# Folded bias vectors of an attention layer: weighted sums over weight chunks on VectorE, one product with ones per output chunk on TensorE

## The chip, the cores and the metric

The kernel runs on one core of one Trainium2 chip. A core has TensorE (PE, matrix products; its weight loads are shown as PEld), VectorE (DVE), ScalarE (ACT), GpSimd (POOL) and SyncE (SP, which here only issues DMAs). The metric is the device time of one launch in microseconds (us). Everything is float32 unless said otherwise.

## The reference

The input x is 8 images of 512 channels by 32 x 32 pixels. Four layers follow each other, each with a residual; only what bears on the change is given.

- Layer 0: an attention over 64 channels, whose score matrix is divided by its largest singular value sigma. Then `conv1x1(z2, Wv, bv) + x`.
- Layer 1, the layer of the change:

```
h = group_norm(x) * gamma + beta
q = wq h + bq;  k = wk h + bk;  v = wv h + bv
out = wp (v softmax(q^T k / sqrt(512))^T) + bp
x = x + out
```

- Layer 2: an attention with 128 channels. Layer 3: a product of signs with sign weights, batch norm and a leaky rectifier.

All weight matrices of layer 1 are 512 x 512, the biases have 512 entries.

## The kernel before

**Folding.** Layer 1 needs neither q nor v. The kernel makes two products of weights, `wu` (from wq and wk) and `wo` (from wv and wp), so that scores are h^T (wu h + bu) and the output is wo h weighted by the softmax, plus bo. The folded biases are `bu` = wk^T bq and `bo` = wp bv + bp, each a vector of 512 held as a tile of 128 partitions by 4 chunks. `bvo` is `bo` plus layer 0's bias.

**Stages.** Up to about 100 us all images are loaded and projected for layer 0 (L1241), weights are turned (`natural`, L1201) and statistics taken. From then to about 194 us one pair of images gets its sigma, by a power iteration (`chain`, L1020 and L1021: two products of 128x128, each result evicted half by DVE, L1036 or L1042, half by ACT, L1034 or L1038; every third step a trace is summed: L1047, L1048 on DVE, a product L1052, and a reciprocal L1075). When it ends (`td`, ln and exp on ACT at L1096 and L1099, each with a load of its table), the pair's weights are made (L287), and the first image goes through `entering(0)`: four visits (L409 on PE; L418, L421 and L423 on DVE), then the group norm's means and variances (L430, L437), the reciprocal root with GpSimd (L232), `normal` (L460) and `split_h` (L324 to L327). The rest of the time to the end is the eight images' main work, from `make_u` on (L385).

**What fills the gaps.** Between the steps of that chain PE does other work, from the generator `filler` (L1411): the product `wu` (L1281), grams of the other three pairs (L1328, after transposes L1133 that are evicted by DVE at L1139 and ACT at L1137), the folded biases (`biases`, L1297), and last the product `wo` (L1281 again, 16 products of 128x512, evicted at L1294). The loop at L1443 takes so many items from the filler at each step of the chain, and the loop at L1450 so many at each visit:

```
    for n in (2, 3, 3, 3, 3, 4, 6):
        next(steps)
        for _ in range(n):
            next(todo, None)
```

PE's order is that of the program there (`manual_schedule`); the other engines' order is set by a planner. Each engine works its own queue in that order. `biases` runs inside the filler, one item after each item of the grams (L1427).

**How a bias is made before.** For each of the four output chunks, four products with a moving operand of one column add up over the four input chunks in one PSUM bank (L1306); DVE then copies the column (L1314) or adds bp (L1316). That is 16 products for bu and 16 for bo.

PSUM in this stage has two double banks (`wide`) and four single ones (`bank`), shared by the chain, the transposes, the visits and the biases.

Of the kernel before, what the change touches and what calls it, by code (L numbers as in the profile page):

```python
# [8 lines left out]
F32 = mybir.dt.float32  # L9
# [3 lines left out]
ALU = mybir.AluOpType  # L13
# [3 lines left out]
P = 128  # L17
B = 8
C = 512
N = 1024  # L20
CC = C // P
# [64 lines left out]
def kernel(  # L86
# [17 lines left out]
    nc = tc.nc  # L104
    mm = nc.tensor.matmul
# [17 lines left out]
    def bank():  # L123
        return psum["bank"].tile([P, HF], F32, tag="bank", name="bank")
# [25 lines left out]
    sbw = {}  # L150

    def load_w(name, src, shape, pool=wpool, eng=nc.sync, tag=None):
        t = pool.tile(shape, F32, tag=tag or name, name=name)
        eng.dma_start(out=t, in_=src)
        sbw[name] = t
        return t
# [4 lines left out]
    a1 = early.enter_context(tc.tile_pool(name="a1", bufs=1))  # L161
# [28 lines left out]
        nc.vector.tensor_tensor(fold[:, i, :], ident[:, 0:MID], ident[:, MID:P], ALU.add)  # L190
    nc.vector.tensor_scalar(fold, fold, 0.5, None, ALU.mult)
    fold = fold.rearrange("p g j -> p (g j)")

    ct = const.tile([P, NCOL], F32, tag="ct", name="ct")
    nc.scalar.dma_start(out=ct, in_=cols)
# [2 lines left out]
    bvc = const.tile([P, CC], F32, tag="bvc", name="bvc")  # L198
# [21 lines left out]
    def vec(name):  # L220
        return ct[:, COL[name] : COL[name] + CC]

    def col(name, i):
        return ct[:, COL[name] + i : COL[name] + i + 1]

    def rsqrt_eps(pool, var, n, name):

        v = pool.tile([P, n], F32, tag=name + "_v", name=name + "_v")
        r = pool.tile([P, n], F32, tag=name + "_r", name=name + "_r")
        e = pool.tile([P, n], F32, tag=name + "_e", name=name + "_e")  # L230
        nc.vector.tensor_scalar(v, var, EPS, None, ALU.add)
        nc.gpsimd.tensor_tensor(r, v, minus_half[:, 0:n], ALU.pow)  # L232
        nc.vector.tensor_tensor(e, r, r, ALU.mult)
        nc.vector.tensor_tensor(e, e, v, ALU.mult)
        nc.vector.tensor_scalar(e, e, -0.5, 1.5, ALU.mult, ALU.add)
        nc.vector.tensor_tensor(r, r, e, ALU.mult)
        return r
# [23 lines left out]
    bu = const.tile([P, CC], F32, tag="bu", name="bu")  # L261
    bo = const.tile([P, CC], F32, tag="bo", name="bo")
# [890 lines left out]
        return absw[:, 0, :]  # L1153

    def scale_signs(total):
        ones = a1.tile([P, 1], F32, tag="ones", name="ones")
        nc.vector.memset(ones, 1.0)
        ps = bank()
        for oc in range(CC):
            mm(  # L1160
                out=ps[:, oc : oc + 1],
                lhsT=total[:, bass.ts(oc, P)],
                rhs=ones,
                start=True,
                stop=True,
            )


        a = rsqrt_eps(a1, vec("L3_conv_bn_var"), CC, "r3")
        nc.vector.tensor_tensor(a, a, vec("L3_conv_bn_gamma"), ALU.mult)  # L1170
        nc.vector.tensor_tensor(cb3, a, vec("L3_conv_bn_mean"), ALU.mult)
        nc.vector.tensor_tensor(cb3, vec("L3_conv_bn_beta"), cb3, ALU.subtract)
        nc.vector.tensor_tensor(cb3, cb3, vec("L3_conv_pr_shift"), ALU.subtract)
        nc.vector.scalar_tensor_tensor(sa3, ps[:, 0:CC], 1.0 / C, a, ALU.mult, ALU.mult)
        a = rsqrt_eps(a1, vec("L2_conv_bn_var"), CC, "r2")
        nc.vector.tensor_tensor(inv2, a, vec("L2_conv_bn_gamma"), ALU.mult)
        nc.vector.tensor_tensor(bb2, inv2, vec("L2_conv_bn_mean"), ALU.mult)
        nc.vector.tensor_tensor(bb2, vec("L2_conv_bn_beta"), bb2, ALU.subtract)

        nc.vector.tensor_tensor(rb3, vec("L3_conv_rsign_bias"), bb2, ALU.add)  # L1180
        nc.vector.tensor_tensor(cb3, cb3, bb2, ALU.add)
        slope = vec("L3_conv_pr_slope")
        nc.vector.tensor_scalar(ps3, slope, -1.0, 1.0, ALU.mult, ALU.add)
        nc.vector.tensor_tensor(pb3, slope, cb3, ALU.mult)
        nc.vector.tensor_tensor(pb3, pb3, vec("L3_conv_pr_bias"), ALU.add)
        nc.vector.tensor_scalar(nc3, cb3, -1.0, None, ALU.mult)
        nc.vector.tensor_tensor(qb3, cb3, vec("L3_conv_pr_bias"), ALU.add)

    def scale_z():

        rep = a1.tile([P, CC, P], F32, tag="absw", name="rep")
        nc.vector.tensor_copy(rep, inv2.unsqueeze(2).to_broadcast([P, CC, P]))
        ps = bank()
        for oc in range(CC):
            mm(out=ps[:, bass.ts(oc, P)], lhsT=rep[:, oc, :], rhs=ident, start=True, stop=True)
        nc.vector.tensor_tensor(sbw["z"], sbw["z"], ps, ALU.mult)


    nat = {}

    def natural(name, tag):  # L1201
        t = nat[name] = a1.tile([P, CC, C], F32, tag=tag, name="nat_" + name)
        for i in range(CC // 2):
            tp = wide().rearrange("p (o c j) -> p o c j", o=2, j=P)
            for k in range(2):
                for cc in range(CC):
                    nc.tensor.transpose(
                        tp[:, k, cc, :], sbw[name][:, cc, bass.ts(2 * i + k, P)], ident
                    )
            dst = t[:, 2 * i : 2 * i + 2, :].rearrange("p o (c j) -> p o c j", j=P)  # L1210
            nc.scalar.copy(dst[:, 0], tp[:, 0])
            nc.vector.tensor_copy(dst[:, 1], tp[:, 1])
            yield
# [62 lines left out]
    def product(lt, rhs, dst, vector):  # L1276
        for i in range(CC // 2):
            ps = wide()
            for k in range(2):
                for oc in range(CC):  # L1280
                    mm(  # L1281
                        out=ps[:, half(k)],
                        lhsT=lt[:, oc, bass.ts(2 * i + k, P)],
                        rhs=rhs[:, oc, :],
                        start=oc == 0,
                        stop=oc == CC - 1,
                    )
                    if k == 0 or oc < CC - 1:
                        yield
            to = dst[:, 2 * i : 2 * i + 2, :].rearrange("p o c -> p (o c)")  # L1290
            if i % 2 and vector:
                nc.vector.tensor_copy(to, ps)
            else:
                nc.scalar.copy(to, ps)  # L1294
            yield

    def biases():  # L1297

        for w, rhs, dst in (
            (nat["k"], [col("L1_conv_bq", k) for k in range(CC)], bu),  # L1300
            (sbw["p"], [bvc[:, k : k + 1] for k in range(CC)], bo),
        ):
            for i in range(CC):
                ps = bank()
                for k in range(CC):
                    mm(  # L1306
                        out=ps[:, 0:1],
                        lhsT=w[:, k, bass.ts(i, P)],
                        rhs=rhs[k],
                        start=k == 0,  # L1310
                        stop=k == CC - 1,
                    )
                if dst is bu:
                    nc.vector.tensor_copy(bu[:, i : i + 1], ps[:, 0:1])  # L1314
                else:
                    nc.vector.tensor_tensor(  # L1316
                        bo[:, i : i + 1], ps[:, 0:1], col("L1_conv_bp", i), ALU.add
                    )
                yield
        nc.vector.tensor_tensor(bvo, bo, vec("L0_conv_bv"), ALU.add)  # L1320


# [2 lines left out]
    def gram(j, i, lt, rhs):  # L1325
        ps = wide()
        for t in range(NT):
            mm(  # L1328
                out=ps[:, 0:P],
                lhsT=lt[:, t, :],  # L1330
                rhs=rhs[:, t, :],
                start=t == 0,
                stop=t == NT - 1,
            )
            if t == NT // 2 - 1:
                yield
        nc.vector.tensor_tensor(gm[j][:, i, :], ps[:, 0:P], mask2, ALU.mult)
        yield
# [30 lines left out]
    ps = bank()  # L1369
# [5 lines left out]
    ps = bank()  # L1375
# [35 lines left out]
    def filler():  # L1411

        yield from natural("v", "k")
        load_w("p", w_p, [P, CC, C], a1, tag="v")
        yield from product(nat["q"], nat["k"], wu, True)
        yield from gram(jl, 2, ht_pair[jl], gtl)
        scale_z()
        yield  # L1420
        between = biases()
        sums = sums_u()
        for j in rest:
            for _ in grams(j):
                next(sums, None)
                yield
                if next(between, "end") != "end":  # L1427
                    yield
        yield from product(nat["v"], sbw["p"], wo, False)

    todo = filler()
    for _ in range(5):
        next(todo)
# [215 lines left out]
```

## Time and profile before

| | us |
|---|---|
| median of 4 runs (1914.26 to 1915.22) | 1914.88 |
| the profiled execution | 1914.82 |
| its span, first to last instruction | 1913.0 |
| busy time of PE / DVE / ACT / POOL | 1891.7 / 1126.3 / 510.3 / 224.3 |
| granted TensorE clock, mean | 0.999 |

The stage around the change, by stretches of the trace (busy us of each engine):

| from to | PE | PEld | DVE | ACT | POOL |
|---|---|---|---|---|---|
| 134.4 to 158.7 | 22.56 | 21.48 | 13.28 | 5.84 | 0.00 |
| 158.7 to 187.0 | 26.89 | 17.66 | 17.46 | 4.37 | 0.00 |
| 187.0 to 198.5 | 10.82 | 4.73 | 9.81 | 2.61 | 1.02 |
| 198.5 to 221.0 | 22.50 | 9.56 | 7.44 | 3.33 | 2.53 |

A line of the chain of waits reads: start in us, length, engine, tile, line, and how many records. A line of the timeline reads: start, length, engine, line, operation, out<-in, count; in brackets, how long the engine had been idle before it and what released it. A float32 product has two records (two passes), a float32 transpose one. The ends of matmul records are modelled, and neighbours overlap; the start-to-start distance is the time that one takes from PE.

### The profile page before, as it was taken

The page shows a single profiled execution, that of the slowest core. Times are in us where ns is not written, and L with a number is a line of the kernel's source. Part 1 is how long each engine was busy: PE and PEld are TensorE (multiplying, and loading weights), DVE is VectorE, ACT ScalarE, POOL GpSimd, SP SyncE. Part 2 cuts the span into 40 slices and gives each one's busy share as a digit, 9 for nine tenths or more (in the row PEclk, how much of TensorE's full clock was granted, in tenths as well). Part 3 has the DMA queues.
Part 4 walks back from the last instruction along what each step waited for, and adds up shares of the span by engine and source line. Part 5 has one row for each costly group of instructions (what it writes and reads, how often), then busy time and mean ns, then how long its engine had stood idle before and what let it go on. Part 6 is the DMA issues. An engine that isn't in the chain of part 4 may idle for free.

```text
span 1913.0 us, 16430 instructions
## 1 busy us (share of the span) xinstructions
PE 1891.7 (99%) x6166; PEld 982.2 (51%) x6166; DVE 1126.3 (59%) x1761; ACT 510.3 (27%) x811; POOL 224.3 (12%) x175
## 2 busy tenths in 40 slices
PE   9999999999999999999999999999999999999997
PEld 3366456544655447454645446544645455544653
DVE  3245677448664677447764676447753775466547
ACT  2141221135212332125212331034202521234014
POOL 0000001200121011200121011201120011101121
PEclk9999999999999999999999999999999999999999
DMA  8420000002000120002000120002000200010001
GB/s 319 159 78 7 0 6 12 1 12 88 17 1 0 33 72 12 0 12 88 17 1 0 34 72 12 1 12 88 11 1 5 94 12 0 0 34 22 12 1 46
DMA packets 27782, 66.45 MB, mean 35 GB/s; under 512 B 4272, under 2 KB 5424, under 8 KB 27056
## 3 DMA queue, kind: packets, MB, share of 16 engines
q1 hardware_dynamic: 26768, 64.90, 10.1%
q8 instruction: 50, 0.82, 0.2%
q10 hardware_dynamic: 864, 0.43, 0.1%
q14 instruction: 36, 0.29, 0.0%
q0 software_dynamic: 64, 0.00, 0.0%
HBM read 38.51 MB, written 18.87 MB: 30 GB/s over the span
## 4 chain that ended last, share of the span: by engine, by line
PE 92%; DVE 6%; issue 1%; ACT 1%; DMA 0%; POOL 0%; DVEq 0%; ACTq 0%
PE bank L385 42%; PE bank L554 20%; PE bank L949 6%; PE bank L803 6%; PE bank L1241 5%; PE bank L655 3%; PE bank L409 2%; PE bank L672 2%; PE wide L1281 1%; DVE both L746 1%; PE wide L1328 1%; DVE both L716 1%; PE bank L1020 1%; PE bank L1021 1%; PE bank L695 1%; PE bank L824 1%
## 5 line engine op out<-in xcount | busy, mean ns | idle before, releaser
L554 PE MATMUL bank<-e,vt 128*128 128x512 f32 x768 | 334.2, 593 | 0.0
L554 PEld LDWEIGHTS bank<-e,vt 128*128 128x128 f32 x768 | 144.9, 190 | 174.8 <-issue 173.1
L385 PE MATMUL bank<-ut,h 128*128 128x512 f32 x384 | 182.3, 597 | 0.0
L342 DVE TENSOR_TENSOR e<-bank,e 128x512 f32<-128x512 f32 x128 | 87.8, 686 | 81.9 <-PE bank L385 81.7
L385 PE MATMUL bank<-us,hs 128*128 128x512 f32 x256 | 121.5, 597 | 1.3 <-DVE us L314 0.5
L385 PEld LDWEIGHTS bank<-ut,h 128*128 128x128 f32 x384 | 71.4, 190 | 95.6 <-issue 84.0
L949 PE MATMUL bank<-e,tpg 128*128 128x512 f32 x256 | 114.7, 595 | 0.0
L803 PE MATMUL bank<-tpg 128*128 128x512 f32 x256 | 114.6, 592 | 0.0
L810 ACT ACTIVATE e<-bank 128x512 f32<-128x512 f32 x128 | 76.4, 597 | 128.6 <-PE bank L803 128.6
L385 PE MATMUL bank<-wo,h 128*128 128x256 f32 x384 | 91.8, 382 | 0.0
L815 DVE TENSOR_TENSOR esum<-esum,e 128x1024 f32<-128x1024 f32 x48 | 58.8, 1225 | 54.8 <-ACT e L810 54.8
L385 PE MATMUL bank<-h,wu 128*128 128x512 f32 x192 | 90.3, 593 | 0.7 <-ACT ut L347 0.7
L357 POOL TENSOR_TENSOR e<-e 128x512 f32<-128x512 f32 x32 | 43.3, 1354 | 403.9 <-ACT e L336 238.3
L949 PEld LDWEIGHTS bank<-e,tpg 128*128 128x128 f32 x256 | 48.1, 190 | 63.2 <-issue 63.1
L803 PEld LDWEIGHTS bank<-tpg 128*128 128x128 f32 x256 | 48.6, 190 | 60.7 <-issue 60.5
L385 PEld LDWEIGHTS bank<-wo,h 128*128 128x128 f32 x384 | 71.6, 190 | 13.5 <-ACT vt L336 4.1
L357 POOL TENSOR_TENSOR ut<-ut 128x512 f32<-128x512 f32 x16 | 21.8, 1361 | 478.1 <-ACT ut L338 478.1
L342 DVE TENSOR_TENSOR vt<-bank,vt 128x512 f32<-128x512 f32 x64 | 44.1, 688 | 56.2 <-PE bank L385 55.9
L385 PEld LDWEIGHTS bank<-us,hs 128*128 128x128 f32 x256 | 47.1, 190 | 54.9 <-issue 48.3
L832 DVE RECIPROCAL rsum<-bank 128x512 f32<-128x512 f32 x15 | 50.4, 3358 | 38.2 <-PE bank L824 38.2
L683 ACT ACTIVATE sg<-xt,rb 128x512 f16<-128x512 f32 x64 | 45.0, 718 | 103.7 <-DVE xt L674 100.2
L1241 PE MATMUL bank<-xt,fg 128*64 128x512 f32 x256 | 59.8, 615 | 4.3 <-DMA fg<-in_w_fg 4.3
(328 smaller groups left out, 3022.3 us busy)
## 6 DMA issues: line engine op xcount, KB each, us to landing
xt<-in_x SPq DMA_DIRECT2D x55, 512.0 KB
out<-both SPq DMA_DIRECT2D x63, 256.0 KB
rfull<-rsum SPq DMA_DIRECT2D x60, 128.0 KB
f_dram<-f SPq DMA_DIRECT2D x8, 256.0 KB
fb<-f_dram SPq DMA_DIRECT2D x8, 256.0 KB
w<-in_w SPq DMA_DIRECT2D x1, 1024.0 KB
q<-in_w_q SPq DMA_DIRECT2D x1, 1024.0 KB
k<-in_w_k SPq DMA_DIRECT2D x1, 1024.0 KB
```

Of the source, the lines that this page charges most:

```text
L342: nc.vector.tensor_tensor(dst, ps, u, ALU.add)
L357: nc.gpsimd.tensor_tensor(c22, c22, c12, ALU.add)
L385: mm(out=ps[:, q * w : (q + 1) * w], lhsT=lt(ka, kb, q, k), rhs=rhs(ka, kb, q, k), start=first and q == 0 and k == 0, stop=last and k == 1 ...
L554: mm(out=ps, lhsT=a[:, t, bass.ts(r_, P)], rhs=e[t], start=first and t == 0, stop=last and t == NTH - 1, skip_group_check=True,)
L655: mm(out=ps[:, i, :], lhsT=xt[:, cc, bass.ts(4 * h + i, P)], rhs=sbw["tpg"][:, cc, 2 * P : 3 * P], start=cc == 0, stop=cc == CC - 1,)
L683: nc.scalar.activation(sg[:, cc, :], xt[:, cc, half(h)], AF.Sign, bias=rb3[:, cc : cc + 1])
L803: mm(out=ps, lhsT=pt[:, 0, bass.ts(t, P)], rhs=tt[:, 0, half(h)], start=True, stop=True,)
L810: nc.scalar.activation(e[:, half(h)], ps, AF.Exp, scale=float(P) ** -0.5)
L815: nc.vector.tensor_tensor(esum, esum, e, ALU.add)
L832: nc.vector.reciprocal(r, ps)
L949: mm(out=banks[h], lhsT=gt[:, t, :], rhs=es[t][:, half(h)], start=t == 0, stop=t == NT - 1,)
L1241: mm(out=banks[i][side(h), :], lhsT=w0[i][:, cc, :], rhs=xt[:, cc, half(h)], start=cc == 0, stop=cc == CC - 1,)
```

## The change

The sums over the four input chunks move from PE's accumulation to DVE. For each of the two biases DVE multiplies the first chunk of the matrix by its bias column, one value per partition, and then adds the other three chunks, multiplied likewise (`tensor_scalar` once, `scalar_tensor_tensor` three times, 128x512 each). What is left, the sum over the 128 partitions, is one product with a column of ones for each output chunk: four products into four columns of one bank, evicted by one DVE instruction. The tile `part` takes the place of tile `absw`. The ones vector is now made once, early, by GpSimd, and shared with `scale_signs`.

`biases` yields False after each step that gives PE nothing, and True after a group of products; the filler then makes an item of its own only for True. So the filler has two items of biases and not eight, and what stands behind them moves up against the chain's steps. The first image's and all later main work keeps its order on all engines.

```diff
+    ones1 = a1.tile([P, 1], F32, tag="ones", name="ones1")
+    nc.gpsimd.memset(ones1, 1.0)
...
     def scale_signs(total):
-        ones = a1.tile([P, 1], F32, tag="ones", name="ones")
-        nc.vector.memset(ones, 1.0)
...
-                rhs=ones,
+                rhs=ones1,
...
     def biases():
-        for w, rhs, dst in (
-            (nat["k"], [col("L1_conv_bq", k) for k in range(CC)], bu),
-            (sbw["p"], [bvc[:, k : k + 1] for k in range(CC)], bo),
-        ):
+        part = a1.tile([P, 2, C], F32, tag="absw", name="part")
+        for j, (w, v) in enumerate(((nat["k"], vec("L1_conv_bq")), (sbw["p"], bvc))):
+            t = part[:, j, :]
+            for k in range(CC):
+                if k == 0:
+                    nc.vector.tensor_scalar(t, w[:, 0, :], v[:, 0:1], None, ALU.mult)
+                else:
+                    nc.vector.scalar_tensor_tensor(
+                        t, w[:, k, :], v[:, k : k + 1], t, ALU.mult, ALU.add
+                    )
+                yield False
+        for j, dst in enumerate((bu, bo)):
+            ps = bank()
             for i in range(CC):
-                ps = bank()
-                for k in range(CC):
-                    mm(
-                        out=ps[:, 0:1],
-                        lhsT=w[:, k, bass.ts(i, P)],
-                        rhs=rhs[k],
-                        start=k == 0,
-                        stop=k == CC - 1,
-                    )
-                if dst is bu:
-                    nc.vector.tensor_copy(bu[:, i : i + 1], ps[:, 0:1])
-                else:
-                    nc.vector.tensor_tensor(
-                        bo[:, i : i + 1], ps[:, 0:1], col("L1_conv_bp", i), ALU.add
-                    )
-                yield
+                mm(
+                    out=ps[:, i : i + 1],
+                    lhsT=part[:, j, bass.ts(i, P)],
+                    rhs=ones1,
+                    start=True,
+                    stop=True,
+                )
+            if dst is bu:
+                nc.vector.tensor_copy(bu, ps[:, 0:CC])
+            else:
+                nc.vector.tensor_tensor(bo, ps[:, 0:CC], vec("L1_conv_bp"), ALU.add)
+            yield True
         nc.vector.tensor_tensor(bvo, bo, vec("L0_conv_bv"), ALU.add)
...
                 next(sums, None)
                 yield
-                if next(between, "end") != "end":
+                if next(between, None):
                     yield
```

## The prediction

> **What bounds the kernel now.** I read the page first: the busy line, then the chain that ended last.
>
> ```profile
> span 1913.0 us, 16430 instructions
> PE 1891.7 (99%) x6166; PEld 982.2 (51%) x6166; DVE 1126.3 (59%) x1761; ACT 510.3 (27%) x811; POOL 224.3 (12%) x175
> PE 92%; DVE 6%; issue 1%; ACT 1%; DMA 0%; POOL 0%; DVEq 0%; ACTq 0%
> ```
>
> TensorE is the bound over the whole span. But the change touches 65 us only: PE's order is the same in both programs up to 134.4 us (the products of `scale_z` and one power step) and again from the first product of `make_u` (L385, 194.1 us). So the forecast is how much earlier that second point comes. The chain in this stretch, piece by piece (start, us, what):
>
> ```profile
> 144.49 0.79 PE bank L1306 x8
> 145.28 0.33 PE bank L1020 x2
> 145.61 0.22 PE bank L1021 x2
> 145.83 0.89 PE wide L1328 x8
> ...
> 157.29 0.29 DVE td L1048
> ...
> 158.40 0.30 DVE td L1048
> 158.70 0.04 issue
> 158.75 0.38 PE bank L1052 x2
> 159.13 3.68 PE wide L1328 x32
> ...
> 182.77 0.22 DVE mv L423
> 182.99 0.02 issue
> 183.01 0.17 DVE mv L429
> 183.18 0.04 issue
> 183.23 0.39 PE bank L430 x2
> 183.61 3.54 PE wide L1281 x8
> 187.15 0.12 PE bank L437 x2
> 187.27 6.97 PE wide L1281 x16
> ```
>
> Two things are woven here. One is a latency line: ten power steps (L1020/L1021, each needing DVE's and ACT's eviction of the last), then sigma (158.75), pair weights (L287, 162.74), four layer-0 visits (L409, the last at 178.71), the means (L430, 183.23), the variances (L437, 186.99), then `normal` and `split_h` on DVE. The other is PE filler put between its steps: biases, grams (L1328), transposes, the products for `wo` (L1281). Where filler fills every gap, less PE work is less time; where it doesn't, the line decides. The DVE timeline shows the line's end:
>
> ```profile
> 187.31 0.16 DVE L231 TENSOR_SCALAR r_v<-bank 128x4 f32<-128x4 f32 x1 [2.91 <-PE bank L437]
> 190.10 3.74 DVE L460 TENSOR_SCALAR h<-xt,r_r,bi 128x512 f32<-128x512 f32 x8
> 195.00 1.23 DVE L325 TENSOR_TENSOR hs<-h,hs 128x1024 f32<-128x1024 f32 x1
> ```
>
> The first h chunk is there 3.65 us after L437 starts (190.10 + 0.54 - 186.99), the second operand T2 9.24 us after it (196.23). PE asks for T2 only at 198.46, so today 2.2 us of slack lie there, made by eight `wo` products (6.97 us) behind L437.
>
> **Removed and returned on PE.** The eight L1306 groups, from their start to the next PE start, take 0.92, 0.91, 0.90, 0.81, 0.82, 0.81, 0.81 and 0.89: 6.87 us. What follows one starts slowly (L1020 0.30 against 0.22, L1328 0.98 against 0.89): seven times 0.08, 0.6. Together 7.5 us for 32 products; 8 come back, two groups, 1.9. Net 5.6 us less PE work. [...] The granted clock is 1.00 here.
>
> **Added on DVE.** Two scalar multiplies of 128x512 (nearest row L460: 0.54 us, 0.47 apart; L707 0.42) and six scalar_tensor_tensor of 128x512 with SBUF operands (L716: 741 to 753 ns), each dependent on the last: 2 x 0.5 + 6 x 0.75 = 5.5 us, against eight evictions of 0.16 that become two (-1.0). DVE is busy 13.3 of 24.3 us from 134.4 to 158.7, so there is room, but DVE works in its order, and the adds stand in front of evictions that the power steps wait for. Upper bound for one: L746, the same operation, ranges up to 1517 ns. [...] The trace has POOL busy 0.00 us from 134.4 to 158.7, and its one operation up to 194 is L232 at 187.55. I take 0.75.
>
> **The ones vector.** A memset moves from DVE (0.06 us at 0.81 us, nobody waiting) to POOL's queue in front of its first DMA issue at 1.29 us: 0.04 to 0.12 us later (L211's memset) for `bhc`, which is needed after the first image's products. Nothing.
>
> **The order.** `biases` now yields False while DVE adds, so grams move up: between two power steps PE does a gram half where it did a bias group. No wait for a transfer is added that is late: matrix p, which DVE now reads from about 141 us and not PE from 146.6, was issued at 103.40, and the DMA engines carry at most 2 GB/s from 120 to 150 us.
>
> **Walk through the ten steps** with these durations, both programs at 134.41: f transposes at 135.0 as now. The g transposes' bank now waits for the scaled eviction L1042, behind the first multiply and the last su sum on DVE: 136.6, a stall of 0.6 (now 0.35 at L1306). Then steps start at (now): 137.6 (137.37), 138.9 (138.76), 141.2 (141.16), 143.8 (143.78; a stall of 0.2 as now), 145.2 (145.14), 147.5 (147.38), 150.1 (149.83; the second bias group may wait 0.3 for ACT's scaled eviction), 151.6 (151.25), 153.9 (153.49), 156.3 (156.11). So the steps do not come closer: the PE time taken out is filled with grams at once. The last step to sigma's product is shorter: now 2.64 us with the 0.68 eviction gt (157.49) between the two td sums, afterwards a gm of 0.29 there, about 2.1. Sigma at 158.4, now 158.75: 0.3 gained, with 24 gram products (24 x 0.234 = 5.6 us) done ahead that now follow.
>
> **From sigma to the variances.** Now L287 comes 3.99 us after sigma, behind 16 gram products (3.75) which just cover ln, the second table load and exp. Afterwards an ft eviction (0.59) stands on ACT between ln and that table load (1.28): the weights are ready at 4.4, PE's cover is 16 transposes and 8 grams (0.24 + 1.8 + 1.9 = 3.9), stall 0.4. L287 at 162.8: nothing gained (162.74). Then PE adds up: L287 1.06, 8 grams 1.97, L409 1.06, 8 grams 1.97, one L1281 0.87, and three times L409 1.06 with three L1281 (2.67) between two: the last L409 starts at 177.2. Now 178.71. The stall of 0.72 before the third pair's transposes (169.13) is gone. L430 follows the last L409's start by 4.52 (183.23 - 178.71), DVE's visit; three L1281 cover 2.67 of it, so PE stalls 0.8. L430 181.7, L437 3.76 later: 185.5, now 186.99: 1.5 gained.
>
> **The tail.** Only two L1281 are left behind L437 (1.8 us). h is late next: PE waits until 185.5 + 3.65 = 189.2, does two terms with the eviction of 0.6 between, and waits for T2 until 185.5 + 9.3 = 194.8. Now that product starts at 198.46, so 2.1 us of slack turn into gain. In sum 1.5 + 2.1 = 3.6, less 0.1 for slow starts after stalls: 3.5 us. Behind, order and waits are the same in both programs and PE was closed up to 219 us, so the shift stays to the end.
>
> The profiled execution took 1914.82 us (span 1913.0 and 1.8 around it): 1911.3. The median of the runs, 1914.88, is 0.06 above it: **1911.4 us**.
>
> **Rivals.** (1) All of the PE time is gained, 5.6 us: 1909.3. The busy share of 99% speaks for it; DVE's fixed 9.2 us behind L437 with 1.8 us of cover speaks against. (2) The line is later than I walked: evictions stand behind two adds instead of one, or banks free later at steps that the trace can't show. Each add in front of a step costs its excess over its cover; at 1.1 us an add, if five of six reach the line (an estimate from the walk), 5 x 0.35 = 1.7, gain 1.8: 1913.1. Against it, 0.75 us is stable in 56 records of L716. (3) Slower: DVE becomes the line's bound. Every add beyond 0.75 is paid about five times; at 1.5 us (the end of L746) 3.8 us are lost and 1915.2 results, at 2.4 us 8.2 are lost: 1919.6. It decides against the change from 1.45 us an add, and by 0.2% from 2.2. For it: six adds in one queue with the steps. [...]
>
> **How the numbers follow.** 0.2% is 3.8 us, about what a measurement of this kernel can tell from no change. The likeliest case has 0.60 with its own range 1910.6 to 1912.0 (the 0.4 us doubts at bias bank, gm and means); a third of it is beyond 3.8 us, for the sum lies 0.3 short of that bound. Rival 1 (and between) 0.10, rival 2 0.20, rival 3 0.10. Faster 0.2 + 0.1 = 0.3, slower 0.1, within 0.6. The range runs from 1909.8 (most of rival 1) to 1914.8 (all gain absorbed).
>
> **What would show it.** Right: 8 one-column records of 107 ns a group twice instead of eight times; six adds at 0.75; sigma near 158.4; L409's last pair near 177.2; PE stalls of about 0.8 before the means, 1.9 before h, 1.2 before T2. Wrong: adds of 1 us or more; sigma later than 159; no wait for h (then the line got shorter, or PE later); a shift that changes behind 200 us.

## The result and the profile after

The changed kernel takes 1911.18 us (median of 35 runs, 1910.07 to 1912.06) against 1914.56 us (55 runs, 1913.48 to 1915.72): the ratio is 0.9982, with a 95% interval of 0.9977 to 0.9987. That is 3.4 us or 0.18% less: clear of the noise, for the interval ends below 1, but a little less than the 0.2% from which the prediction speaks of a faster kernel. The profiled execution took 1911.42 us, its span 1909.5. Two runs that took far longer at a low mean clock (the kernel before once 3311.79 us at 0.562, e6 once 1989.15 us at 0.947) are left out of every figure here.

The page of the changed kernel, span and busy line:

```profile
span 1909.5 us, 16334 instructions
PE 1886.2 (99%) x6118; PEld 972.6 (51%) x6118; DVE 1130.1 (59%) x1762; ACT 510.3 (27%) x811; POOL 224.5 (12%) x176
```

PE is busy for 5.5 us less than before (1891.7) and has 48 records less. So 5.5 us of PE work went, and 3.5 us of span. The other 2 us are in the list of PE's waits between 134 and 200 us, first of the kernel before, then of the changed one (line that waits, what it waits for, us in total, times, longest):

```profile
PE bank L1052 <- DVE td L1048: 1.1, 1, 1.1
PE quad L1133 <- DVE xt L418: 0.7, 1, 0.7
PE bank L385 <- ACT ut L347: 0.7, 1, 0.7
PE bank L430 <- DVE mv L429: 0.6, 1, 0.6
...
```

```profile
PE bank L387 <- DVE h L462: 1.7, 1, 1.7
PE bank L387 <- DVE hs L327: 0.9, 1, 0.9
PE bank L1054 <- DVE td L1050: 0.7, 1, 0.7
PE bank L387 <- ACT ut L349: 0.7, 1, 0.7
PE bank L432 <- DVE mv L431: 0.6, 1, 0.6
...
```

With the small ones left out here (0.3 and 0.3; 0.4, 0.3 and 0.2) PE waited 3.7 us before and waits 5.5 afterwards. The two new waits on top are those for h (L462) and for T2 (hs, L327), the second operand that `split_h` makes. Lines of the changed kernel stand 2 further down than before up to `scale_signs`, at their old numbers from there to `biases`, and 7 further down behind it; L387 is the old L385, L439 the old L437, L1281 is the same.

The chain of waits of the changed kernel has turned at its end. Where the kernel before had 16 records of `wo` products on PE (187.27, 6.97 us), the chain now runs through POOL and DVE:

```profile
185.51 0.13 PE bank L439 x2
...
185.67 0.17 DVE r_v L233
...
185.91 1.03 POOL r_r L234
...
188.46 3.73 DVE h L462 x8
192.20 1.15 DVE hs L326
...
193.36 1.24 DVE hs L327
...
194.64 5.42 PE bank L387 x12
```

**One ruler for all kernels.** The stage is measured in each trace from the last product that all orders share (L1052 or L1054 with `tj`, at 134.41 us before and 134.07 after) to the product that takes T2 (the third group of L385 or L387, at 198.46 and 194.64). This takes out the first 134 us, which differ between executions by about 1 us. From that length I subtract PE's waits as that list gives them, and half of the time within it in which the granted clock was a half and PE did not wait (in e1 below the same four records take 3.78 us there and not 1.98, so half of that time is lost); the rest is PE's work at full clock.

| kernel (us; the experiments follow below) | length | waits of PE | lost at half clock | rest | median of runs |
|---|---|---|---|---|---|
| before | 64.05 | 3.7 | 0 | 60.4 | 1914.56 |
| after | 60.57 | 5.5 | 0 | 55.1 | 1911.18 |
| e1 no sums | 61.15 | 6.3 | 2.5 | 52.4 | 1912.44 |
| e2 PE sums, two items | 68.55 | 5.4 | 3.4 | 59.8 | 1922.31 |
| e3 DVE sums, old pace | 64.43 | 6.2 | 3.4 | 54.8 | 1914.72 |
| e4 adds twice | 64.40 | 7.5 | 1.7 | 55.2 | 1914.72 |
| e5 visits closer | 56.73 | 2.3 | 0 | 54.4 | 1906.92 |
| e6 before, visits closer | 62.89 | 3.1 | 0 | 59.8 | 1913.04 |
| e8 no sums, padded | 59.81 | 4.5 | 0 | 55.3 | 1910.22 |
| e9 two more behind | 60.58 | 3.8 | 0 | 56.8 | 1910.68 |
| e10 PE sums, four items | 65.25 | 3.7 | 1.7 | 59.9 | 1915.54 |
| e11 old pace, padded | 61.64 | 4.7 | 0 | 56.9 | 1912.05 |

The rest falls into two groups: about 60 us where PE makes the sums, about 55 where DVE does (57 with the 1.75 us of padding of e9 and e11; e1 is lower by the products that it leaves out, some 1.9 us, and e8 has 2.6 us of padding on top of that). So the ledger closes within about 1 us: a kernel's time in this stage is PE's work, plus what PE waits, plus what its clock loses. The medians stand 1850.1 to 1850.6 us above the lengths, except for e1 (1851.3) and e2 (1853.8), where other runs lost more clock than the profiled one.

### The profile page after: what moved, and what is told of

The parts are those of the page before. It is cut to its first block, busy times and chain, and to the rows that moved or that the text cites. A ratio compares the mean times of both kernels' runs of the same rounds, so it can differ in the third digit from the quotient of the medians.

```text
span 1909.5 us, 16334 instructions
## 1 busy us (share of the span) xinstructions
PE 1886.2 (99%) x6118; PEld 972.6 (51%) x6118; DVE 1130.1 (59%) x1762; ACT 510.3 (27%) x811; POOL 224.5 (12%) x176
## 4 chain that ended last, share of the span: by engine, by line
PE 92%; DVE 7%; issue 1%; ACT 1%; DMA 0%; POOL 0%; DVEq 0%; ACTq 0%
PE bank L387 42%; PE bank L556 20%; PE bank L951 6%; PE bank L805 6%; PE bank L1241 5%; PE bank L657 3%; PE bank L411 2%; PE bank L674 2%; DVE both L748 1%; DVE both L718 1%; PE wide L1281 1%; PE wide L1335 1%; PE bank L1022 1%; PE bank L1023 1%; PE bank L697 1%; PE bank L826 1%
## 5 line engine op out<-in xcount | busy, mean ns | idle before, releaser
L387 PE MATMUL bank<-ut,h 128*128 128x512 f32 x384 | 182.3, 597 | 0.0
L387 PE MATMUL bank<-us,hs 128*128 128x512 f32 x256 | 121.5, 597 | 1.3 <-DVE us L316 0.5
L387 PEld LDWEIGHTS bank<-ut,h 128*128 128x128 f32 x384 | 71.4, 190 | 95.6 <-issue 84.0
L387 PE MATMUL bank<-h,wu 128*128 128x512 f32 x192 | 90.4, 593 | 2.4 <-DVE h L462 1.7
L387 PE MATMUL bank<-wo,h 128*128 128x256 f32 x384 | 91.8, 382 | 0.0
L817 DVE TENSOR_TENSOR esum<-esum,e 128x1024 f32<-128x1024 f32 x48 | 58.8, 1226 | 54.8 <-ACT e L812 54.8
L387 PEld LDWEIGHTS bank<-wo,h 128*128 128x128 f32 x384 | 71.6, 190 | 13.5 <-ACT vt L338 4.1
L387 PEld LDWEIGHTS bank<-us,hs 128*128 128x128 f32 x256 | 47.1, 190 | 54.9 <-issue 48.3
```

What stands on the lines that cost most here:

```text
L387: mm(out=ps[:, q * w : (q + 1) * w], lhsT=lt(ka, kb, q, k), rhs=rhs(ka, kb, q, k), start=first and q == 0 and k == 0, stop=last and k == 1 ...
L817: nc.vector.tensor_tensor(esum, esum, e, ALU.add)
```

## The experiments

**e1: no sums at all.** The body of `biases` is replaced; wk^T bq and wp bv are left out of bu and bo.

```diff
-        part = a1.tile([P, 2, C], F32, tag="absw", name="part")
-        ...
-            yield True
+        nc.vector.tensor_copy(bu, vec("L1_conv_bq"))
+        nc.vector.tensor_copy(bo, vec("L1_conv_bp"))
+        yield False
```

> The changed kernel without the folded sums: bu is a copy of bq's chunk columns and bo of bp's, so wk^T bq and wp bv are left out, with their six adds, two multiplies and eight products with ones. PE has about 1.9 us less to do than in the changed kernel and 7.5 us less than in the kernel before; four wo products come before the means' product and one (of 0.9 us) less group stands behind the variances' product. Theory (the latency line from the power steps over sigma, visits, means, variances to h and T2 sets the end of this stage): little or nothing more is gained than by the change, 1909.5 to 1912 us, 2.9 to 5.4 us below the kernel before; the wait of PE for h grows beyond 1.7 us. Rival (PE's work decides): all 7.5 us are gained, 1907.1 us. Rival (the adds on DVE hold the power steps): sigma's product comes 1 us or more earlier than in the changed kernel and the time falls below 1909.

Measured: 1912.44 us (1910.11 to 1914.46), ratio 0.9991 (0.9984 to 0.9998). So taking the whole of the sums away, on PE and on DVE, is no better than moving them. PE's timeline of e1 (start, length, engine, line, operation, then in brackets the idle time before it and what ended it) and its windows (span of time, busy us of PE, PEld, DVE, ACT and POOL with counts, granted clock, DMA share, GB/s):

```profile
187.85 2.61 PE L387 MATMUL bank<-h,wu 128*128 128x512 f32 x4 [3.52 <-DVE h L462]
191.14 3.78 PE L387 MATMUL bank<-h,wu 128*128 128x512 f32 x4 [0.68 <-ACT ut L349]
194.71 2.44 PE L387 MATMUL bank<-hs,su 128*128 128x512 f32 x4
```

```profile
184.00:188.00 4.00, 0.48 (x4) 0.37 (x3) 2.14 (x10) 1.01 (x1) 1.02 (x1) 1.00 0.00 0
188.00:192.00 4.00, 3.32 (x5) 1.00 (x6) 4.00 (x8) 0.59 (x1) 0.00 (x0) 0.63 0.00 0
192.00:196.00 4.00, 4.00 (x6) 1.68 (x5) 3.53 (x4) 0.69 (x1) 0.00 (x0) 0.52 0.00 0
```

The wait for h grew to 3.52 us, as the latency line demands. But something came on top that I had not expected: the same group of four records takes 3.78 us instead of 1.98, and the clock column falls to 0.63 and 0.52. (4 x 0.37 + 4 x 0.48 = 3.4 us of clock are missing, that is 6.8 us at one half, the last 1.1 of them behind the start of T2's product.) The four runs with a mean clock of 0.999 took 1910.11 to 1910.94 us; the others, at 0.995 to 0.997, 1911.7 to 1914.5. Rival "PE's work decides" (1907.1) is out; the median lies above the expected range. The four runs without the fall lie in it, of the sixteen others only five, at its upper end.

**e2: the order of the change with PE's sums.** The 32 one-column products of before, in two items of 16.

```diff
+        for _ in range(8):
+            yield False
         for w, rhs, dst in (
...
-                yield
+            yield True
...
-                if next(between, "end") != "end":
+                if next(between, None):
```

> The order of the change without its saving: the 32 one-column products of the kernel before stay on PE, but in two items of sixteen, where the changed kernel has its two groups of four products; the grams move up as in the change. Theory: PE has its 5.6 us of work back, in two lumps of 3.4 us that stand in front of power steps, and the wo products behind the variances' product are as few as in the changed kernel; so the stage ends about 5 us later than with the change and later than before: 1915.5 to 1917.5 us. Rival (the change of order alone brings the gain, the work removed from PE is beside it): at or below the kernel before, 1911.5 to 1914.6 us.

Measured: 1922.31 us (1919.44 to 1923.0), ratio 1.0043 (1.0026 to 1.0059), 5 us above the expected range. PE's timeline and the windows of e2:

```profile
145.93 3.70 PE L1308 MATMUL bank<-ct,nat_k 128*128 128x1 f32 x32
149.49 0.78 PE L1020 MATMUL bank<-cur 128*128 128x128 f32 x2
...
152.51 3.76 PE L1308 MATMUL bank<-bvc,p 128*128 128x1 f32 x32
156.13 0.74 PE L1020 MATMUL bank<-cur 128*128 128x128 f32 x2
```

```profile
144.00:149.00 5.00, 5.00 (x48) 5.00 (x47) 2.17 (x8) 1.09 (x3) 0.00 (x0) 1.00 0.02 3
149.00:153.00 4.00, 4.00 (x24) 4.00 (x24) 1.65 (x6) 0.61 (x2) 0.00 (x0) 0.57 0.00 0
153.00:156.00 3.00, 3.00 (x29) 3.00 (x29) 0.47 (x3) 0.34 (x1) 0.00 (x0) 1.00 0.00 0
156.00:160.00 4.00, 4.00 (x23) 4.00 (x23) 1.11 (x5) 0.39 (x2) 0.00 (x0) 0.57 0.00 0
```

PE counts as fully busy in all these windows, and still the clock falls behind each lump of one-column products (the fall starts within 0.15 us of the lump's end, before or after it). Two causes are mixed in this run, the order and the clock, so it could not answer the question of the order; e10 repeats it.

**e3: the saving without the order.** Each step of `biases` counts as an item again, so the grams stay where they were.

```diff
-                if next(between, None):
+                if next(between, "end") != "end":
                     yield
```

> The saving of the change without its order: DVE makes the sums and PE two groups of products with ones, but each of the ten steps of the biases counts as an item of the filler as in the kernel before, and eight of the ten give PE nothing; so the grams do not move up between the power steps, and more wo products are left behind the variances' product. Theory: the freed PE time now makes the power steps shorter where there was filler and nothing else, sigma's product comes 1 to 3 us earlier than in the changed kernel, and the wo products behind the variances' product cover the waits for h and T2, which the changed kernel shows as 1.7 and 0.9 us: 1909 to 1910.5 us, faster than the changed kernel by 1 to 2 us. Rival (DVE's and ACT's evictions hold the steps, so less filler only makes idle PE): the steps stay where they are and the grams left out come back behind sigma, 1912 to 1914.5 us.

Measured: 1914.72 us (1913.87 to 1915.36), ratio 1.0002 (0.9993 to 1.0011): all of the gain is gone, and the time is 4 to 6 us above what was expected. The steps did get shorter: from the shared product to sigma's product 20.98 us pass (133.45 to 154.43), 3.03 less than in the changed kernel (134.07 to 158.08), and no wait for h or T2 is left. Two things took the gain back. The steps stand in bare stalls (2.1 us for ACT's scaled eviction in three places, 1.6 before sigma), and after the last of them the clock falls, as the windows show:

```profile
150.00:154.00 4.00, 2.66 (x23) 2.34 (x22) 2.63 (x10) 2.40 (x4) 0.00 (x0) 1.00 0.00 0
154.00:158.00 4.00, 3.57 (x18) 3.60 (x19) 1.69 (x6) 1.47 (x3) 0.00 (x0) 0.57 0.01 2
158.00:162.00 4.00, 4.00 (x19) 3.77 (x21) 1.37 (x7) 0.81 (x2) 0.00 (x0) 0.58 0.00 0
```

**e4: each addition twice.** Chunks 1 to 3 are added two times.

```diff
-                    nc.vector.scalar_tensor_tensor(
-                        t, w[:, k, :], v[:, k : k + 1], t, ALU.mult, ALU.add
-                    )
+                    for _ in range(2):
+                        nc.vector.scalar_tensor_tensor(
+                            t, w[:, k, :], v[:, k : k + 1], t, ALU.mult, ALU.add
+                        )
```

> The changed kernel with each of the six scalar_tensor_tensor additions executed twice, so chunks 1 to 3 are added twice; DVE has 4.5 us more to do among the power steps, and is busy about 22 of 24 us there. Theory (each add stands in front of an eviction that a power step waits for, and is paid beyond some cover): the cost is 1.5 to 4.5 us on the changed kernel, 1912.7 to 1915.7 us, and sigma's product comes that much later. Rival (DVE has room, 17.7 of 24.3 us are busy, and the adds lie in its idle time): within 0.7 us of the changed kernel, 1910.5 to 1912 us.

Measured: 1914.72 us (1914.21 to 1917.26), ratio 1.0005 (0.9996 to 1.0014): 3.5 us above the changed kernel. The rival "DVE has room" is out. Sigma comes 27.83 us after the shared product (133.68 to 161.51) where the changed kernel needs 24.01. Of these 3.8 us, 1.7 are again the clock (0.66 over 5 us behind a new stall of 1.56 us). So 4.5 us of added DVE work cost about 2.1 us on the line (what is left of 3.8 when the 1.7 are taken off).

```profile
146.92 0.47 PE L1022 MATMUL bank<-cur 128*128 128x128 f32 x2
...
149.17 0.38 PE L1054 MATMUL bank<-tj,mask 128*128 128x1 f32 x2 [1.56 <-DVE ft L1141]
...
154.04 0.63 PE L1022 MATMUL bank<-cur 128*128 128x128 f32 x2
```

**e5: less filler between the visits.** The products that this leaves over come behind the variances (L439).

```diff
-        for n in (2, 3, 3, 3, 3, 4, 6):
+        for n in (2, 2, 2, 2, 4, 2, 6):
```

> The changed kernel with fewer filler products between the four visits: 2, 2, 2, 2, 4, 2, 6 items in place of 2, 3, 3, 3, 3, 4, 6; the work is the same, but six wo products and not two stand behind the variances' product. Theory (after sigma the latency line sets the end, because visits are spaced by filler and the last waits have none): PE's waits after sigma of 0.6 (means), 1.7 (h) and 0.9 us (T2) go, the one of 0.7 us for the eviction stays; 1907.4 to 1908.6 us, about 3 us below the changed kernel, and then PE's work is the bound. Rival (the visits cannot come closer, for DVE needs 2.8 us of work for each and the spacing is 3.7 now): the waits move to the visits, 1910 to 1911.5 us.

Measured: 1906.92 us (1906.07 to 1907.47, 5 runs), ratio 0.9961 (0.9948 to 0.9975). It beats both kernels: 7.5 us below before, 4.3 below the changed one, 0.5 better than expected. PE's timeline of e5:

```profile
178.49 0.30 PE L432 MATMUL bank<-mv,gmat 128*128 128x4 f32 x2
...
180.46 0.28 PE L439 MATMUL bank<-dev,gmat 128*128 128x4 f32 x2
180.59 5.40 PE L1281 MATMUL wide<-p,nat_v 128*128 128x512 f32 x12
185.83 1.88 PE L387 MATMUL bank<-h,wu 128*128 128x512 f32 x4
188.38 1.98 PE L387 MATMUL bank<-h,wu 128*128 128x512 f32 x4 [0.68 <-ACT ut L349]
190.20 1.88 PE L387 MATMUL bank<-hs,su 128*128 128x512 f32 x4
```

No bracket is left at L432, at the first L387 and at T2: six `wo` products stand behind L439 and cover h. The visits now follow each other at 3.0 us (L411 at 164.91, 167.95, 170.92, 173.90), where DVE works without a gap.

**e6: the same spacing in the kernel before.**

```diff
-        for n in (2, 3, 3, 3, 3, 4, 6):
+        for n in (2, 2, 2, 2, 4, 2, 6):
```

> The kernel before, with the same fewer items between the visits (2, 2, 2, 2, 4, 2, 6). Theory: there PE's work sets the end of this stage already (2.2 us of slack before T2), so only some of its own waits can be won, 0.7 before a transpose and 0.6 before the means: 1913.2 to 1914.5 us. The difference to the changed kernel with the same spacing is then 5 to 6.5 us, the whole of the PE time that the change removes, where with the old spacing it is 3.4. Rival (closer visits are worth the same in both kernels): 1911 us or less, and a difference of about 3.4.

Measured: 1913.04 us, ratio 0.9993 (0.9985 to 1.0002). There the spacing is worth about 1.5 us, because twelve `wo` products (10.55 us, from 181.97) now stand behind L437 and PE is late, not h. Between e6 and e5 lie 6.1 us: with that spacing DVE's sums are worth all of the PE work (5.4 us in the ledger) and 0.8 us of waits (3.1 against 2.3), where with the old spacing they are worth 3.4.

**e8: e1 with padding.** Three products that nobody reads, behind L439, where PE stood idle for 3.5 us. The folded sums are left out as in e1.

```diff
         for _ in todo:
             pass
+        ps = bank()
+        for i in range(3):
+            mm(
+                out=ps,
+                lhsT=nat["v"][:, i, 0:P],
+                rhs=sbw["p"][:, i, :],
+                start=i == 0,
+                stop=i == 2,
+            )
```

> The kernel without the folded sums (they are left out, as in the first experiment), with three products of 128x512 for nothing (2.6 us, into a bank that nobody reads) behind the variances' product, where PE stood idle for 3.4 us and the granted clock then fell to a half for 6 us. Theory (the idle stretch makes the clock fall, and the latency line covers the added work): the clock stays at 1.00 in this stage and all runs lie at 1910.0 to 1911.0 us, although PE does 2.6 us more. Rival (PE's work decides): 1913 us or more. Rival (the clock falls for another reason): runs spread up to 1914 us as before.

Measured: 1910.22 us (1909.45 to 1911.27), ratio 0.998 (0.9972 to 0.9988). With 2.6 us more PE work the kernel is 2.2 us faster than e1, every run has a mean clock of 0.998 or 0.999, and the spread of e1 is gone. The windows of e8 at the same place:

```profile
184.00:188.00 4.00, 4.00 (x12) 1.61 (x10) 1.19 (x8) 1.01 (x1) 1.02 (x1) 1.00 0.00 0
188.00:192.00 4.00, 2.48 (x6) 0.97 (x6) 3.99 (x11) 0.58 (x1) 0.00 (x0) 1.00 0.00 0
192.00:196.00 4.00, 3.12 (x8) 1.21 (x7) 3.97 (x5) 0.69 (x1) 0.00 (x0) 1.00 0.00 0
```

So the idle stretch (3.52 us before h in e1, 0.84 here) brought the clock down in e1, and the line hides work that is put there. It also shows what leaving out the sums is worth without that disturbance: 1.0 us below the changed kernel, for 1.9 us of PE work and 5.5 us of DVE work less (the undisturbed runs of e1, 1910.1 to 1910.9, say the same).

**e9: two more products in the changed kernel.** The same padding, two products (1.75 us), on the changed kernel.

```diff
+        ps = bank()
+        for i in range(2):
+            mm(
+                out=ps,
+                ...
+            )
```

> The changed kernel with two more products of 128x512 for nothing (1.75 us of PE time, into a bank that nobody reads) behind the variances' product, where PE waits 1.70 us for h. Theory (the end of this stage is set by the line from the variances to h and T2): nothing to 0.2 us is lost, 1911.0 to 1911.5 us. Rival (PE's work decides): 1.75 us are lost, 1912.9 us.

Measured: 1910.68 us (1910.17 to 1911.86), ratio 0.9981 (0.9974 to 0.9988), not slower than the changed kernel's 1911.18. PE's timeline of e9:

```profile
185.90 1.96 PE L1281 MATMUL wide<-p,nat_v 128*128 128x512 f32 x4
187.70 1.88 PE L1465 MATMUL bank<-p,nat_v 128*128 128x512 f32 x4
189.56 1.96 PE L387 MATMUL bank<-h,wu 128*128 128x512 f32 x4
192.19 1.98 PE L387 MATMUL bank<-h,wu 128*128 128x512 f32 x4 [0.68 <-ACT ut L349]
195.06 1.98 PE L387 MATMUL bank<-hs,su 128*128 128x512 f32 x4 [0.88 <-DVE hs L327]
```

The useless products (L1465) take exactly the place of the wait of 1.70 us, and the stage is 60.58 us long against 60.57. So PE's work no longer decides at that point.

**e10: e2 in four items of eight products.**

```diff
-        for _ in range(8):
+        for _ in range(6):
             yield False
...
-            yield True
+                if i % 2:
+                    yield True
```

> As the second experiment (the 32 one-column products stay on PE and the grams move up), but in four items of eight products, 1.8 us each, not in two of sixteen, behind which the granted clock fell to a half. Theory (two causes were mixed there: PE's 5.6 us of work, and a clock that falls when PE does one-column products for 3.5 us on end): the clock stays at 1.00 in this stage, and the time is that of PE's work, 1913.5 to 1916 us, at or a little above the kernel before and 2.5 to 5 us above the changed kernel. Rival (order alone brings the gain of the change): 1910.5 to 1912 us. Rival (the loss of the second experiment came from the order and not from the clock): 1918 us or more.

Measured: 1915.54 us (1913.33 to 1919.75), ratio 1.0008 (1.0001 to 1.0015). The expectation for the time holds, the one for the clock doesn't: it fell in this arrangement too (3.4 us at one half, 151.3 to 154.7 us), so the median agrees in part by luck. The windows of e10:

```profile
146.00:150.00 4.00, 3.80 (x35) 3.57 (x34) 2.01 (x9) 0.74 (x2) 0.00 (x0) 1.00 0.00 0
...
152.00:154.00 2.00, 2.00 (x11) 2.00 (x11) 0.55 (x2) 0.27 (x1) 0.00 (x0) 0.50 0.00 0
```

The runs lie in three heaps: 3 at 1913.3 to 1913.8 with a mean clock of 0.998, 13 at 1915.2 to 1916.0 with 0.997, 4 at 1919.3 to 1919.8 with 0.996. The first heap tells what the order with PE's sums is worth undisturbed: about 0.8 us below before and 2.4 above the changed kernel. So the order alone makes about a quarter of the gain, and the sums that PE no longer does make the rest.

**e11: e3 with padding.** Two products that nobody reads (1.75 us), behind the first group of products with ones.

```diff
             if dst is bu:
+                pad = bank()
+                for i in range(2):
+                    mm(
+                        out=pad,
+                        lhsT=nat["q"][:, i, 0:P],
+                        rhs=nat["k"][:, i, :],
+                        start=i == 0,
+                        stop=i == 1,
+                    )
                 nc.vector.tensor_copy(bu, ps[:, 0:CC])
```

> The third experiment (sums on DVE, the pace of before) with two products of 128x512 for nothing (1.75 us, into a bank that nobody reads) behind the first group of products with ones, where PE stood idle for 1.58 us before sigma's product and the granted clock then was a half from 154.3 to 161.5 us. Theory (the third experiment lost its gain by that clock, 7.2 us at half speed being 3.6 us of work, set off by a stretch of transposes, one-column products and idle time): the clock stays at 1.00 and the time is 1910.5 to 1912 us, 2.5 to 4 us below the third experiment although PE does 1.75 us more. Rival (its gain went to stalls of the steps, and the clock is beside it): 1914.5 to 1916.5 us.

Measured: 1912.05 us (1911.21 to 1912.56), ratio 0.9988 (0.9982 to 0.9995), 2.7 us below e3 with more work. The windows of e11:

```profile
150.00:154.00 4.00, 3.81 (x32) 3.33 (x31) 2.58 (x11) 1.97 (x4) 0.00 (x0) 1.00 0.00 0
154.00:158.00 4.00, 4.00 (x30) 3.20 (x29) 2.63 (x11) 2.15 (x4) 0.00 (x0) 1.00 0.01 2
```

The clock was most of e3's loss (by e3's own trace the half clock lasts 6.8 us, from 154.6 to 161.4, not the 7.2 of the expectation, and costs 3.4). But e11 stays 0.9 us above the changed kernel: its 10 `wo` products behind L439 leave no wait for h or T2, and the stalls of the steps (2.1 + 0.5 + 0.4 us) stand in their place. With either order PE waits for about 5 us of this stage (4.7 and 5.5); what differs is the place. The 1.75 us of padding were not quite free: against e3 the ledger has 1.5 us of waits less and 2.1 us of the rest more.

## Why the prediction was right

The forecast was 1911.4 us, the median is 1911.18; the sum's own figure of 3.5 us is the 3.48 by which the ruler became shorter. Four lines of the changed kernel, three of the timeline of PE and one of the windows:

```profile
158.08 0.38 PE L1054 MATMUL bank<-td,mask 128*128 128x2 f32 x2 [0.70 <-DVE td L1050]
...
162.18 1.41 PE L289 MATMUL bank<-wv,gm 64*128 64x512 f32 x4
163.53 2.05 PE L1335 MATMUL wide<-gt 128*128 128x128 f32 x16
```

```profile
134.40:158.70 24.30, 22.67 (x196) 21.82 (x197) 17.70 (x59) 6.68 (x17) 0.00 (x0) 1.00 0.00 1
```

Step by step, with 0.34 us added to each time of the changed kernel, by which its trace is earlier at the shared product:

- **Net PE work, 5.6 us:** 5.5 on the page, 5.3 in the ledger, 5.4 between the rests of e6 and e5. The two groups of ones take 0.82 and 0.91 us to the next start, as the eight did: about 103 and 114 ns a record, where the eight gave 107 (6.87 us for 64 records).
- **The adds, 0.75 us each:** 741 to 754 ns for the six, 476 and 478 for the two multiplies. No run shows an add of 2.4 us, the higher of rival 3's two prices. POOL is busy 0.00 us from 134.4 to 158.7 again, so no add stood beside work of POOL.
- **The ten steps:** predicted from 137.6 to 156.3, seen from 137.45 to 156.21, none off by more than 0.3. Grams filled the freed time. Sigma was forecast at 158.4 and comes at 158.42.
- **Sigma to variances:** pair weights 162.52 (162.8 predicted). The stall of 0.4 stands inside them and not before: they take 1.35 us to the next start (162.18 to 163.53), 0.3 more than the 1.06 of before. Last visit 177.41 (177.2), for three L1281 between two visits take 2.77 us and not 2.67. Means 181.93 (181.7), the stall before them 0.61 (0.8), variances 185.69 (185.5).
- **The tail:** waits of 1.70 for h and 0.88 for T2 (1.9 and 1.2 predicted), T2 at 194.98 (194.8). These are the 0.2 us by which the variances are late. e9 shows that PE's work there is free, e5 that the same saving is paid in full once other work covers the line.
- **Behind:** the shift is 3.82 us at T2 by raw times and 3.70 at 219.77, and stays at 3.70 to 3.72 through all images.

Rival 1 (all of PE's time, 5.6 us) fell with e1, e8 and e9; it becomes true only with e5's spacing. Rival 2 (the line later than walked) did not occur.

That the figure agrees to 0.1 us is in part luck: errors of 0.1 to 0.3 us of both signs stand behind it. Two things beside the sum were wrong. The price of longer adds, "paid about five times" beyond 0.75 us, was too high: e4 added 0.75 us to each of six, and 2.1 us of that reached the line, not 3.8. The rest of e4's loss was the clock. And the clock is the case that the rivals lacked. The prediction saw a granted clock of 1.00 in the trace of before and took it for granted in the trace of after; that it held there was not reasoned. In the traces of five of the ten variants it fell in this very stage. The changed kernel stays clear of it (mean clock 0.998 or 0.999 in each run), but not by much: one stall of 1.56 us more between its steps (e4), or 1.8 us more of waiting at the end (e1), was enough. The slower case should have been that one, at 1.7 us for each 3.4 us at one half, and not adds of 1.5 us.

## What to carry to other kernels

PE work that is removed pays only where PE's own order is what comes last; count what covers the latency line behind the removed work, and look for filler that can be put back into the new gap. Here the change alone gave 3.4 us, and the change with fewer fillers between the visits 7.5. When filler is moved or removed around a latency line, check the granted clock of that stage in the trace and over several runs before the order is blamed: here a kernel with less to do was slower (e1, 1912.44 us against 1911.18), and useless products made it faster (e8, 1910.22; e11, 2.7 us below e3).

## What the runs showed of the hardware

**The half clock came in stretches of 3.4 us.** In every trace where it fell in this stage, the time at one half was 3.4 us or twice that: 3.4 in e4 (0.34 x 5 us = 1.7 us missing) and in e10 (151.3 to 154.7), twice 3.4 in e2 (0.43 x 4 us missing each), 6.8 on end in e3 (154.6 to 161.4) and in e1 (189.0 to 195.8). In e2 the clock changes at 149.36, 152.77, 156.19 and 159.60 us, each 3.41 us after the last (worked out from its granted clock of 0.68, 0.61, 0.59 and 0.70 in the windows of 1 us from 149, 152, 156 and 159). The same kernel falls in one run and not in the next: e10 in 17 of 20 runs by their mean clock (0.996 or 0.997, the others 0.998), e1 in 16 of 20 (0.995 to 0.997, the others 0.999). No run here shows why.

**The clock fell while PE was busy.** It fell not only after idle time: in e2 it fell behind two unbroken lumps of sixteen one-column products, in e10 where lumps of eight alternate with short steps and transposes, while PE and PEld were shown as fully or almost fully busy (5.00 and 5.00 of 5 us from 144 to 149 in e2, 3.80 and 3.57 of 4 us from 146 to 150 in e10). In the kernel before, with the same products in groups of four between grams, it did not fall in the trace (1.00 from 134.4 to 198.5), and the mean clock was 0.998 or 0.999 in every run. The 3.41 us in front of e2's first fall (145.95 to 149.36) hold one-column products and nothing else. In e1 the last 3.4 us in front of the fall (185.6 to 189.0) hold 1.15 us of products of 512 columns. What all these falls have in common was not shown.
